# Folded weight pairs, quantised weight tiles and result buffers placed elsewhere in a two-layer attention and feed-forward kernel

## The chip, the cores and the metric

The kernel runs on one core of a Trainium2 chip. The metric is the device time of one execution in microseconds (us), as the median of three runs. Five engines work beside each other, each through its own list of instructions in order: TensorE (PE, with its weight loads shown as PEld), VectorE (DVE), ScalarE (ACT), GpSimd (POOL) and SyncE (SP), which in this kernel issues nearly all DMAs.

## The reference

The input x has 8 batches of 100 rows of 512 numbers, 800 rows in all. Two layers follow, each made of a cross attention and a feed-forward block that are added to x:

```python
x = x + L0_xattn(layernorm(x), ctx, Wq, Wkv_expand, Wout)      # 16 heads, causal
x = x + L0_ffn(layernorm(x), Wg, W1, W2, W3)                   # 8 experts, best 2 of 8
x = x + L1_xattn(layernorm(x), ctx, Wq, w_kc_q, w_kc_kv, W_qr, W_kr, Wo)
x = x + L1_ffn(layernorm(x), w_gate_up, w_down)                # quantised to 8 bits
```

In the second attention the queries pass through three matrices per head: `q_hk = hidden_q @ Wq.T`, then `w_kc_q` (from 128 to 384 numbers per head), then `W_qr` (from 384 to 64). In the second feed-forward block the rows, both weights and the hidden values are rounded to integers from -127 to 127, with one scale per row: `scale = max|v| / 127`, `q = round(v / scale)`, and `q * scale` is used.

## The kernel before

**Stages.** The 800 rows lie in 7 tiles of 128 (the last has 32). The kernel computes attention 1 batch by batch, then the gate (which two experts each row goes to), then the eight experts one after another on 240 slots each, then attention 2 batch by batch, then the last feed-forward block tile by tile. Each row goes to a slot of an expert through DRAM: `give_slots` works out the slots and POOL scatters the rows into `x_slot` (L686); `fetch` (L1015) reads an expert's slots back; the results are scattered with addition into `x_acc` (L1186).

**Order.** Up to the branch and in the expert loop the order on PE, DVE and ACT is the order in which the code is written (`tc.manual_schedule`). SP and POOL are ordered by a planner, and so is all of attention 2.

**The branch.** If an expert gets more than 240 rows, the rest is computed in a block under `tc.If(spills > 0)`. The number is worked out from the gate (`spilt`, L831), and each engine loads it and branches (L906, L913). In the profiled run the block is skipped.

**Folding.** The three query matrices of attention 2 are multiplied into one, `wqf`, two heads (one pair) at a time, eight pairs in all, as filler work ahead of attention 2. `fold_load(i)` (L698 to L705) brings a pair in by five DMAs from SP: `wq_p` of 512 KB, two `kq_p` of 192 KB and two `qr_p` of 96 KB. Then

- `fold_first` (L711): 6 matrix products of 128x64 on PE (12 records), and a copy to `a_p` by ACT (L719);
- `fold_second` (L749): 2 products of 64x512 (4 records), copied to `f_p` by ACT (L753);
- `fold_third` (L759): 4 transposes, copied to `wqf` by ACT (L760).

In the expert loop `fold_beside` (L731) and `fold_turn` (L741) take the place of `fold_first`. The pool of the loads has three buffers. Pairs 0 and 1 are folded among the gate's instructions ahead of the branch, pairs 2 and 3 directly behind the branch, pairs 4 to 7 in experts 0 to 3.

**The gate's second part.** Rows 640 to 799 (tiles 5 and 6) pass the gate last: statistics, `gate_norm` (L560), `gate_columns` (transposes L578, copies L583 and L581), `gate_scores` (L593, L601), `rank_choices` (a row of some 20 short DVE instructions with one exponential on ACT, L631), `give_slots` (products L658 and L661 on PE, then DVE and the scatters).

**An expert.** `gate_and_up(0)`, `(1)` and `(2)` each do 16 records L1109 on PE, a silu on ACT (L1120, L1128) and the product `hT` on DVE (L1121 to L1133). Then the next expert's rows are transposed (`columns_of`, L1040) and copied to `xgT`, one half by ACT (L1044) and one by DVE (L1042); then `hT` goes through the third weight (L1175), and the results are scaled (L1183, L1185) and scattered.

**Integers of the last block's weights.** Between these, DVE turns weights of the last feed-forward block into integers: `quantise` is a maximum (L147), two short instructions (L135, L138) and two passes (L142, L143), then SP sends the tile through a DMA that transposes it (L152). `quantise_next` does one of 22 gate/up tiles (128x512), twice per expert, and asks for the next (`gu`, L850); `quantise_down` does one of 4 down tiles (128x1408) in experts 0 to 3, between `gate_and_up(1)` and `(2)`, and `load_down` then asks for the next into the same buffer (`dn`, L855). `LATER = 9` of the gate/up tiles are left for attention 2, where up to two per batch from batch 1 on have a place.

**The end.** `finish_rows` scales a result (L1668), adds x (L1671) and sends it out (L1672), in buffers named `y`, of which there are two.

## Time and profile before

| | us |
|---|---|
| median of three runs | 674.64 |
| runs | 672.87 to 675.77 |
| profiled execution | 681.28 |
| its span | 679.5 |
| PE busy | 646.9 (95%) |
| DVE busy | 419.9 (62%) |
| ACT busy | 245.0 (36%) |
| POOL busy | 183.5 (27%) |

The stages of the profiled execution, by their first matrix products: attention 1 to about 105 us, the gate and the branch to 131, folded pairs to 141.6, experts 143.5 to 283, weights of the values and queries to 345, attention 2 to 536, the last block to 679.5.

Below, the page's slices: the span in 40 equal parts of 17 us. Each digit is the busy share of an engine in tenths (9 is 90% or more); PEclk is the clock granted to PE in tenths of full speed; DMA is the mean busy share of the DMA engines.

```profile
PE   8999997889998999999989999999999999999994
...
DVE  4875697326655553353148877876677356666687
ACT  3654544322222111232145555555555313222140
...
PEclk9999999589999999999989999999999999999998
DMA  9700393699999998654200211110000210011211
```

The eighth slice runs from 119 to 136 us, where the gate's second part, the branch and the first folded pairs behind it lie. The DMA engines are busy at 90% or more in the slices of the experts.

A row of a timeline gives the start in us, the length in us, the engine, the line, the operation, what it writes and reads, and in brackets how long the engine was idle before and what ended that.

### The profile page before, as it was taken

Reading aid. Unit: us, or ns where it says so; the run is one execution under the profiler, and the core shown is the slowest. Engines: PE = TensorE matmul, PEld = TensorE weight load, DVE = VectorE, ACT = ScalarE, POOL = GpSimd, SP = SyncE. Lnnn points to the kernel's source line nnn. Section 1 sums busy time; section 2 is a strip of 40 time slices with the busy share of each in tenths; the row PEclk is TensorE's granted clock in tenths of the full one; section 3 lists DMA queues with packets and bytes.
Section 4 is the critical chain, followed back from the end, with each engine's and each line's share of the span. In section 5 each row is a group of like instructions: output and inputs, shape, how many; then the busy total and the mean of one; then the engine's idle time right before and its main releaser. Section 6 shows DMA issues by size and latency. Waiting matters only on the chain.

```text
span 679.5 us, 9904 instructions
## 1 busy us (share of the span) xinstructions
PE 646.9 (95%) x3476; PEld 415.3 (61%) x3483; DVE 419.9 (62%) x1065; ACT 245.0 (36%) x565; POOL 183.5 (27%) x196
## 2 busy tenths in 40 slices
PE   8999997889998999999989999999999999999994
PEld 5766755666655677568866666666666544444442
DVE  4875697326655553353148877876677356666687
ACT  3654544322222111232145555555555313222140
POOL 2222231501110122138514243244234102221020
PEclk9999999589999999999989999999999999999998
DMA  9700393699999998654200211110000210011211
GB/s 292 249 18 17 119 322 108 241 309 220 299 295 302 253 326 214 140 175 120 84 1 15 59 44 21 53 36 12 0 13 0 90 38 20 18 30 29 49 37 63
DMA packets 80290, 80.35 MB, mean 118 GB/s; under 512 B 41267, under 2 KB 54119, under 8 KB 80111
## 3 DMA queue, kind: packets, MB, share of 16 engines
q1 hardware_dynamic: 76543, 70.97, 36.6%
q0 software_dynamic: 3696, 8.72, 6.0%
q8 instruction: 29, 0.48, 0.3%
q14 instruction: 22, 0.18, 0.1%
HBM read 56.36 MB, written 16.50 MB: 107 GB/s over the span
## 4 chain that ended last, share of the span: by engine, by line
PE 63%; DVE 7%; DMA 7%; POOL 1%; issue 1%; ACT 1%; SPq 0%; ACTq 0%; POOLq 0%; DVEq 0%
PE bank L359 12%; PE bank L1406 9%; PE bank L1379 9%; PE bank L1109 8%; PE bank L1325 6%; PE bank L1175 5%; PE bank L1394 5%; PE bank L1539 3%; DMA dn<-in_wdn 2%; PE bank L1361 1%; DMA gu<-in_wgu 1%; DMA qr_p<-in_wqr 1%; POOL e L1388 1%; DVE amax L147 1%; PE bank L711 1%
## 5 line engine op out<-in xcount | busy, mean ns | idle before, releaser
L1388 POOL TENSOR_SCALAR e<-e,rs 128x361 f32<-128x361 f32 (+1 forms) x56 | 67.2, 1201 | 131.9 <-DVE rs L1387 118.7
L359 PE MATMUL bank<-wvo,ctxT 128*128 128x512 f32 x192 | 83.9, 593 | 0.0
L1379 PE MATMUL bank<-kvT,qe 128*128 128x361 f32 (+1 forms) x208 | 83.0, 483 | 0.1
L1109 PE MATMUL bank<-xgT,w 128*128 128x240 f32 (+1 forms) x384 | 76.5, 373 | 1.6 <-ACT xgT L1044 0.9
L1109 PEld LDWEIGHTS bank<-xgT,w 128*128 128x128 f32 (+1 forms) x384 | 64.7, 183 | 14.4 <-issue 5.6
L1406 PE MATMUL bank<-pT,kvr 121*128 121x400 f32 x192 | 70.3, 502 | 1.0 <-DVE pT L80 1.0
L1394 PEld LDWEIGHTS bank<-ident,e 128*121 128x121 f32 (+1 forms) x312 | 48.3, 186 | 34.2 <-POOL e L1388 7.3
L1385 ACT ACTIVATE e<-bank,nm 128x361 f32<-128x361 f32 (+1 forms) x104 | 58.7, 565 | 27.2 <-DVE nm L1381 18.9
L1381 DVE TENSOR_REDUCE nm<-bank 128x1 f32<-128x361 f32 (+1 forms) x104 | 54.9, 528 | 15.8 <-PE bank L1379 14.6
L359 PEld LDWEIGHTS bank<-wvo,ctxT 128*128 128x128 f32 x192 | 36.2, 190 | 43.0 <-issue 42.6
L1186 POOL DMA_INDIRECT x_acc<-y,place x16 | 24.5, 1530 | 129.9 <-ACT y L1185 126.2
L1394 PE MATMUL bank<-ident,e 128*121 128x128 f32 (+1 forms) x312 | 53.0, 280 | 3.1 <-POOL e L1388 3.0
L1556 POOL TENSOR_TENSOR hid<-g,u 128x512 f32<-128x512 f32 (+1 forms) x17 | 20.5, 1216 | 111.0 <-ACT g L1547 74.8
L1175 PE MATMUL bank<-w,hT 128*128 128x512 f32 (+3 forms) x96 | 44.3, 607 | 4.0 <-DVE hT L1133 4.0
L1406 PEld LDWEIGHTS bank<-pT,kvr 121*128 121x128 f32 x192 | 33.9, 190 | 20.2 <-ACT pT L82 0.7
L1325 PE MATMUL bank<-xT,wqf 128*128 128x256 f32 (+1 forms) x192 | 43.8, 389 | 0.7 <-ACT xT L1310 0.7
L82 ACT COPY pT<-bank 121x384 f32<-121x384 f32 (+1 forms) x63 | 28.2, 447 | 42.4 <-PE bank L1394 42.3
L324 POOL TENSOR_TENSOR s<-s,rs 100x800 f32<-100x800 f32 x16 | 24.4, 1522 | 70.0 <-DVE rs L323 30.5
L1325 PEld LDWEIGHTS bank<-xT,wqf 128*128 128x128 f32 x192 | 36.3, 190 | 7.4 <-ACT xT L1310 0.9
L80 DVE COPY ctxT<-bank 128x400 f32<-128x400 f32 (+2 forms) x31 | 17.7, 572 | 37.0 <-PE bank L1325 26.0
L1379 PEld LDWEIGHTS bank<-kvT,qe 128*128 128x128 f32 (+1 forms) x208 | 32.9, 189 | 10.7 <-DVE rs L1387 0.5
L1175 PEld LDWEIGHTS bank<-w,hT 128*128 128x128 f32 (+3 forms) x96 | 16.8, 184 | 25.1 <-issue 16.6
(259 smaller groups left out, 1004.2 us busy)
## 6 DMA issues: line engine op xcount, KB each, us to landing
w<-in_w SPq DMA_DIRECT2D x8, 1408.0 KB
gu<-in_wgu SPq DMA_DIRECT2D x22, 256.0 KB
w<-in_w SPq DMA_DIRECT2D x16, 256.0 KB
wq_p<-in_wq SPq DMA_DIRECT2D x8, 512.0 KB
wo<-in_wo SPq DMA_DIRECT2D x8, 512.0 KB
x_slot<-zeros SPq DMA_DIRECT2D x1, 3840.0 KB
kq_p<-in_wkcq SPq DMA_DIRECT2D x16, 192.0 KB
dn<-in_wdn SPq DMA_DIRECT2D x4, 704.0 KB
```

What stands on the lines that cost most here:

```text
L82: nc.scalar.copy(dst, src)
L359: nc.tensor.matmul(po[:, :D], lhs[:, c, ds(t * P, r)], rhs[:, c, :], start=(c == 0), stop=(c == chunks - 1),)
L1109: nc.tensor.matmul(po, w12_e[:, c, cols], xgT[:, c, :], start=(c == c0), stop=(c == c1 - 1))
L1175: nc.tensor.matmul(py[i][:n], hT[:mr, m, ds(s0, n)], w3_e[:mr, m, :], start=(m == 0), stop=(m == 2))
L1186: d = nc.gpsimd.indirect_dma_start(out=x_acc, out_offset=bass.IndirectOffsetOnAxis(ap=place[:, 0:1], axis=0), in_=y, in_offset=None, compu ...
L1325: nc.tensor.matmul(pq[:, i, :], wqf[:, c, ts(p0 + i, P)], xT[:, c, :], start=(c == 0), stop=(c == KC - 1),)
L1379: nc.tensor.matmul(ps[:r, :L], qe[:, ds(k0, r)], kvT, start=True, stop=True)
L1381: d = nc.vector.tensor_reduce(nm[:r], ps[:r, :L], AX.X, ALU.max, negate=True)
L1385: nc.scalar.activation(e[:r], ps[:r, :L], AF.Exp, bias=nm[:r], accum_out=sm[:r])
L1388: (nc.vector if odd else nc.gpsimd).tensor_scalar_mul(e[:r], e[:r], rs[:r])
L1394: nc.tensor.transpose(pt[:LP, c, :r], e[:r, ds(c * (LP - 1), LP)], ident[:r, :r])
L1406: nc.tensor.matmul(pc[:, :VC], kvr[:, c, :], pT[:, c, :], start=(c == 0), stop=(c == LC - 1))
```

## The change

Four edits, in the same functions:

1. The fold loads have four buffers in place of three. Pairs 0 to 3 are loaded at the start and folded ahead of the branch, in pieces placed among the gate's second part. Pairs 4 and 5 are loaded there and folded behind the branch, now one after the other in their second and third steps. Pairs 6 and 7 are left for experts 0 and 1; both are loaded behind the branch at once.
2. `quantise_down` goes behind `gate_and_up(2)`, and from experts 0 to 3 to experts 1 to 4. `quantise_next`'s second tile still follows it.
3. 13 gate/up tiles are left for attention 2 in place of 9, so 9 are done in the experts.
4. `y` has four buffers.

To make room, the skipped block now uses memory of `x_all` and `xs` for its weights and rows; this is not shown.

```diff
-    fw, close_fw = open_pool("fold_in", bufs=3, side="right")
+    fw, close_fw = open_pool("fold_in", bufs=4, side="right")
...
-    pairs_left = list(range(3, NH1 // 2))
-    loaded = [fold_load(i) for i in range(3)]
+    pairs_left = list(range(4, NH1 // 2))
+    loaded = [fold_load(i) for i in range(4)]
...
-    part = fold_first(*loaded.pop(0))
+    pair0 = fold_first(*loaded.pop(0))
     project_add(5, po)
...
-    part = fold_second(*part)
+    pair0 = fold_second(*pair0)
     loaded.append(fold_load(pairs_left.pop(0)))
+    pair1 = fold_first(*loaded.pop(0))
     xT = gate_columns(5, 7)
-    fold_third(*part)
+    pair1 = fold_second(*pair1)
+    loaded.append(fold_load(pairs_left.pop(0)))
     gate_scores(5, 7, xT)
 
-    part = fold_first(*loaded.pop(0))
+    pair2 = fold_first(*loaded.pop(0))
+    fold_third(*pair0)
+    fold_third(*pair1)
     rank_choices(5, 7)
     give_slots(5, 7)
...
-    part = fold_second(*part)
-    fold_third(*part)
+    pair2 = fold_second(*pair2)
+    pair3 = fold_first(*loaded.pop(0))
+    fold_third(*pair2)
+    pair3 = fold_second(*pair3)
+    fold_third(*pair3)
...
-    LATER = 9
+    LATER = 13
...
-    while len(loaded) < 3:
+    behind_branch = [loaded.pop(0) for _ in range(2)]
+    while pairs_left:
         loaded.append(fold_load(pairs_left.pop(0)))
...
-    part = fold_first(*loaded.pop(0))
-    following = fold_first(*loaded.pop(0))
-    part = fold_second(*part)
-    following = fold_second(*following)
-    fold_third(*part)
-    fold_third(*following)
+    pair4, pair5 = fold_first(*behind_branch[0]), fold_first(*behind_branch[1])
+    pair4 = fold_second(*pair4)
+    fold_third(*pair4)
+    pair5 = fold_second(*pair5)
+    fold_third(*pair5)
...
-        if e < KC:
+        gate_and_up(2)
+        if 0 < e <= KC:
             turn_down(*quantise_down(*down_in))
-            if e + 1 < KC:
-                down_in = load_down(e + 1)
-        gate_and_up(2)
+            if e < KC:
+                down_in = load_down(e)
...
-        y = f2w.tile([P, D], F32, tag="y", name="y")
+        y = f2w.tile([P, D], F32, tag="y", name="y", bufs=4)
```

More of the change, by code (lines that the diff above doesn't have):

```diff
@@ L937, in tile_kernel @@
             )
+        w12_at = x_all.rearrange("p t w -> p (t w)")[:, : KC * 2 * HE]
+        w12_at = w12_at.rearrange("p (c h) -> p c h", c=KC)
         at_w = sp.tile([P, KC + 3], I32, tag="at_w", name="at_w")
@@ L953, in tile_kernel @@
             nc.gpsimd.iota(at_x, pattern=[[0, 1]], base=0, channel_multiplier=1)
-            w12_e = sp.tile([P, KC, 2 * HE], F32, tag="spw", name="spw")
+            w12_e = w12_at
             for c in range(KC):
                 gathered(w12_e[:, c, :], w12.rearrange("e d h -> (e d) h"), at_w[:, c : c + 1])
-            w3_e = sp.tile([P, 3, D], F32, tag="sp3", name="sp3")
+            w3_e = xs[1:4]
             for m, (m0, mr) in enumerate(HCH):
                 gathered(
-                    w3_e[:mr, m, :], w3.rearrange("e h d -> (e h) d"),
+                    w3_e[m][:mr], w3.rearrange("e h d -> (e h) d"),
                     at_w[:mr, KC + m : KC + m + 1],
@@ L965, in tile_kernel @@
             with tc.For_i(0, NT, 1, hint_engines=()):
-                x_t = sp.tile([P, D], F32, tag="spx", name="spx")
+                x_t = xs[4]
                 gathered(x_t, x_all_rows, at_x)
@@ L991, in tile_kernel @@
                     nc.tensor.matmul(
-                        py[:, :D], hT[:mr, m, :], w3_e[:mr, m, :], start=(m == 0), stop=(m == 2)
+                        py[:, :D], hT[:mr, m, :], w3_e[m][:mr], start=(m == 0), stop=(m == 2)
                     )
-                y_t = sp.tile([P, D], F32, tag="spy", name="spy")
+                y_t = xs[5]
                 nc.vector.tensor_scalar(y_t, py[:, :D], g_t, None, ALU.mult)
@@ L1092, in tile_kernel @@
     nc.scalar.activation(most, ln_eps, AF.Silu)
-    part = fold_first(*loaded.pop(0))
-    following = fold_first(*loaded.pop(0))
-    part = fold_second(*part)
-    following = fold_second(*following)
-    fold_third(*part)
-    fold_third(*following)
+    pair4, pair5 = fold_first(*behind_branch[0]), fold_first(*behind_branch[1])
[3 more added lines that the diff above has]
+    fold_third(*pair5)
+    part = None
     turned = columns_of(0, slots[0])
@@ L1665, in finish_rows @@
         if y is None:
-            y = f2w.tile([P, D], F32, tag="y", name="y")
+            y = f2w.tile([P, D], F32, tag="y", name="y", bufs=4)
         scale = swb[:, OT * P :]
@@ L1735, in tile_kernel @@
         finish_rows(u, pd, s)
-    y = f2w.tile([P, D], F32, tag="y", name="y")
+    y = f2w.tile([P, D], F32, tag="y", name="y", bufs=4)
     for cols in (slice(0, D // 2), slice(D // 2, D)):
```

## The prediction

> **What bounds it now.** I read the slices of the page first: TensorE (PE) is busy nearly everywhere, so a gain must be PE work removed or a stall removed. One stretch breaks the rule, where PEclk falls to 5. I then asked for busy time in windows of 3.41 us laid on that fall. Columns: window; its length; busy us of PE, PEld, DVE, ACT, POOL; granted clock; DMA share; GB/s.

> ```profile
> 114.27:117.68 3.41, 1.30 (x6) 0.28 (x5) 2.77 (x12) 2.15 (x4) 2.21 (x2) 1.00 0.45 122
> 117.68:121.09 3.41, 2.90 (x16) 2.13 (x20) 1.19 (x3) 2.38 (x5) 2.61 (x3) 0.50 0.97 287
> ...
> 131.33:134.75 3.42, 3.42 (x18) 3.42 (x17) 0.00 (x0) 1.07 (x3) 0.27 (x1) 0.50 0.34 82
> 134.75:138.16 3.41, 3.41 (x14) 2.06 (x15) 0.00 (x0) 0.27 (x1) 0.00 (x0) 0.50 0.76 234
> 138.16:141.57 3.41, 3.41 (x14) 1.71 (x11) 0.00 (x0) 1.67 (x3) 0.00 (x0) 0.50 1.04 324
> 216.67:220.08 3.41, 0.98 (x3) 0.49 (x4) 3.19 (x9) 0.00 (x0) 0.00 (x0) 1.00 1.10 345
> 220.08:223.49 3.41, 3.41 (x7) 1.78 (x6) 2.86 (x10) 0.69 (x1) 1.69 (x2) 0.50 1.04 397
> 667.22:670.63 3.41, 2.26 (x23) 1.79 (x24) 3.34 (x7) 0.48 (x1) 0.00 (x0) 1.00 0.02 5
> 670.63:674.05 3.42, 1.28 (x12) 0.89 (x10) 2.69 (x5) 0.00 (x0) 0.00 (x0) 1.00 0.41 153
> ```

> The chain of waits and the timeline give the other stalls:

> ```profile
> 131.02 5.37 PE bank L711 x24
> 136.48 4.65 DMA gu<-in_wgu
> 141.14 7.44 DMA qr_p<-in_wqr
> ```

> ```profile
> 213.39 1.62 DVE L147 TENSOR_REDUCE amax<-dn 128x1 f32<-128x1408 f32 x1 [4.69 <-DMA dn<-in_wdn]
> 219.10 2.85 PE L1175 MATMUL bank<-w,hT 96*128 96x512 f32 x4 [2.88 <-DVE hT L1133]
> 234.00 0.67 DVE L147 TENSOR_REDUCE amax<-gu 128x1 f32<-128x512 f32 x1
> 236.07 0.62 DVE L1042 COPY xgT<-bank 128x448 f32<-128x448 f32 x1
> 237.89 9.23 PE L1109 MATMUL bank<-xgT,w 128*128 128x240 f32 x48
> 672.71 0.75 DVE L1668 SCALAR_TENSOR_TENSOR y<-bank,sh,swb 128x512 f32<-128x512 f32 x1 [0.66 <-DMA out_y<-y]
> ```

> In experts 2 and 3 the down weights arrive late, DVE waits for them in its order, and the products hT behind them hold PE's L1175.

> **Pairs moved ahead of the experts.** The stretch from 115.92 (end of pair 0's L749) to 141.63 (first L1040), 25.7 us, held pair 0's third and pairs 1 to 3; now it holds pair 0's third and pairs 1 to 5, two more. A pair there costs PE, at half clock, 2.82 (L711) + 1.98 (L749) + 1.11 (L759) = 5.9 us; at full clock 1.52 + 1.08 + 0.55 = 3.15 (the last from transposes L578, 20 in 2.74). Two pairs: 11.8 or 6.3. Second and third now follow each other pair by pair, so three thirds wait for their f_p copy (ACT 0.58 and handing over): +2.0. Filled: pair 1's L711 lies in the 2.27 us in which PE waited for x_all at 115.92 to 118.19 (-1.5), and pair 3's L711 in the 0.7 before 128.89. At half clock throughout: 25.7 + 11.8 + 2.0 - 1.5 - 0.7 = 37.3, so L1040 starts at 153.2. At full clock throughout I add the same list in order and reach 140.2 (branch 1.0 us as at 130.02 to 131.02).

> Queued behind the new pieces: pair 1's a_p copy (0.27) stands before the gT copy on ACT, and two wqf copies stand before the exponential of rank_choices. At full clock both fit where DVE's chain ends anyway. At half clock L711 and two L759 (5.0 us) end after DVE wants L658 and the exponential: some 3.8 us for spilt, the last scatters on POOL and SP's fetch of slots (at 134.54); PE's folds are later still, so these cost nothing more. On SP two more fold loads run before the branch, among scatters; their 1.1 MB each may delay the fetch by 0 to 2 us; I take 0, since DMA is at 0.3 to 0.6 from 128 to 136.

> Cover: expert 0's L731 waited 0.29 + 0.91 us for pair 4's qr_p, landed at 148.6. Pair 6 takes its place in the queue behind the same bytes. So being early is worth nothing, and of being late 1.2 us are free.

> **Does the clock hold?** [...] Counting streamed columns (L711 at 46%), the dropped window holds 1.1 us and the one kept at 667.22 some 1.8. The new order offers about 1.8 over the old gap, 1.5 to 1.6 in windows between 119 and 124, and 0.9 to 1.3 across the branch (0.75 + 1.0 us of gaps, then 24 L711). I go by the rows: the clock is lost, most likely before the branch. In the middle of that stretch (122.8 instead of 117.68) 2.6 us run at full clock, and L1040 starts at 150.6: +9.0, less cover 1.2, plus 0.9 for half a slow window left in expert 0: **+8.7**.

> **Experts 1 to 4.** Pairs leave experts 2 and 3. The down integers take DVE 3.92 us (213.39 to 217.31) and now stand after hT, but still before the second gate/up tile (2.04) and L1042, which every L1109 of the next expert needs. After hT at 234.05: 3.92 + 2.04 + 0.62 ends at 240.6, while PE wanted 237.89: a new stall of 2.8 us in experts 2 and 3. In expert 1 pair 7's pieces give PE 1.3 us more: 1.5. In expert 4 no gate/up tile is left for the second place: 0.8. From windows set on L1109's starts, these experts took 17.45, 19.59, 21.67, 16.13 = 74.8 us, and a plain one (the next) 15.21. New: 18.95 + 18.0 + 18.0 + 16.0 = 70.9, **-3.9**. A 2.8 us gap puts a window under the limit in about 7 of 10 phases, at 1.7 us each (220.08): +2.4 for two. So -1.5 net (bounds -3.9 and -0.5). Expert 0 loses its down integers' wait: -0.25. The down tiles land 6 to 9 us after issue and have over 11 us from one use to the next, so I take them as in time; late ones cost 0 to 2.

> **Attention 2** takes four more gate/up tiles on DVE. Batch 2 with two tiles took 21.71 us, batch 6 with none 21.72 (between the context transposes L1285), batch 4 with one 21.99: +0.2 (0 to 0.6). Experts 4 to 6, which lose them, had PE unbroken: 0.

> **Result buffers.** The wait behind y's DMA is 0.66 us of DVE at the end, where DVE sets it: -0.66; the 2.00 us that the chain gives to that DMA overlaps the work before.

> **Sum**: +8.7 - 1.5 - 0.25 + 0.2 - 0.66 = +6.5. The profiled execution took 681.28 us with a span of 679.5; the median of the runs is 674.64, and I carry the difference over to it: 681.1.

> **Rivals.**
> - The clock falls only at the branch (24 L711 stream too little). L1040 at about 145.3: +3.7 - 1.2 + 0.9, the rest -2.2: +1.2, 675.8. For it: the thin windows there. Against: those at 119 to 124 are hardly fuller.
> - Faster: the clock holds to the experts. It decides if 0.9 to 1.3 us of streaming in a window suffices, or if busy time is what counts (1.6 us or more in any window). Nothing is gained before 148.6, so -2.2: 672.4; and if the 2.8 us gaps miss the grid too, 670.0. Against: the rows above; for: the dropped windows all had an idle of over 2 us.

> **Chances.** Lost before the branch 0.5, at it 0.28, held 0.22. Runs may differ, the grid being free of the kernel's start. The range leaves out the lower part of the last case and the worst of the first (all at half clock and late tiles): 671.5 to 685; the forecast's own is 677 to 685. This kernel's measurement tells 0.5% (3.4 us) from no change: faster 0.2 (half the held case, and some for a stall that I overrate), same 0.25, slower 0.55.

> **What would show it.** Right: PEclk at 5 over several slices between 120 and 152, first L1040 near 150; L1109 waiting for DVE xgT L1042 by 2 to 3 us in experts 2 and 3; no DVE wait for dn; no wait for out_y. Wrong: full clock through the branch, or L1109 starting on time because the down integers or the gate/up tile end sooner than PE's L1175.

## The result, and the profile after

The changed kernel took **682.67 us** (median of four runs, 680.47 to 686.76), the kernel before 673.75 us on the same chip (672.33 to 675.77): ratio **1.0124, 95% interval 1.0088 to 1.0161**, slower by some 8.9 us. The two profiled executions lie nearer together: spans of 679.5 us before and 682.8 us after. That gap between the profiled pair and the timed runs is a finding of its own, taken up below.

First the ahead-of-the-experts stretch: busy time of the changed kernel in windows on the grid of its clock changes (in this profile all of them, the later ones at 225.46, 228.87, 358.58, 361.99 and 679.43, lie whole multiples of 3.41 us apart). The columns are as before: window, length, busy us of PE, PEld, DVE, ACT, POOL, granted clock, DMA share, GB/s.

```profile
116.24:119.65 3.41, 2.55 (x22) 2.11 (x20) 2.40 (x6) 2.43 (x5) 2.65 (x3) 1.00 0.87 236
119.65:123.06 3.41, 2.84 (x15) 0.54 (x13) 0.29 (x1) 1.70 (x5) 2.64 (x3) 0.50 1.02 345
...
126.48:129.89 3.41, 3.41 (x23) 2.32 (x22) 1.14 (x11) 1.54 (x4) 1.58 (x2) 0.50 1.04 389
129.89:133.30 3.41, 3.37 (x22) 1.96 (x20) 2.37 (x15) 1.44 (x3) 1.66 (x2) 1.00 0.57 213
133.30:136.72 3.42, 1.84 (x15) 1.63 (x15) 0.00 (x0) 2.55 (x4) 1.19 (x2) 1.00 0.49 154
136.72:140.13 3.41, 3.41 (x18) 3.21 (x18) 0.00 (x0) 0.49 (x2) 0.00 (x0) 0.50 0.57 175
```

The clock is lost at 119.65, although PE was busy for 2.55 of the 3.41 us ahead of it and never idle for more than 0.86 us in a row. It comes back for two windows at 129.89, which was not foreseen, and is lost again at 136.72 until 153.78. The first columns of slots (L1050, before L1040) start at 147.08 in place of 141.63, and expert 0's first L1120 (before L1109) at 149.80 in place of 143.53: 6.3 us later.

Next the chain of waits in the experts (start, us, what). "Issue" is time for which this view names no cause.

```profile
187.22 1.36 issue
188.58 9.31 PE bank L1120 x48
...
204.03 2.68 issue
206.70 9.31 PE bank L1120 x48
...
222.15 2.68 issue
224.83 10.99 PE bank L1120 x48
...
241.96 0.60 issue
```

Four new stalls stand just ahead of the next expert's L1120. The third also costs clock: 10.99 us for 48 products instead of 9.31, with a granted clock of 0.50 from 225.46 to 228.87. The timeline of VectorE around the second stall tells its cause (start, us, engine, line, operation):

```profile
199.63 0.40 DVE L1144 TENSOR_TENSOR hT<-silu,up 64x240 f32<-64x240 f32 x1
199.96 1.60 DVE L147 TENSOR_REDUCE amax<-dn 128x1 f32<-128x1408 f32 x1
...
203.78 0.68 DVE L147 TENSOR_REDUCE amax<-gu 128x1 f32<-128x512 f32 x1
...
205.98 0.62 DVE L1052 COPY xgT<-bank 128x448 f32<-128x448 f32 x1
```

Behind the last hT stand the down weights' integers (199.96 to 203.78), a gate/up tile (to 205.98), and only then L1052, whose columns the L1120 at 206.70 needs. No wait for dn is left on VectorE. At the end of the kernel y's products no longer wait for out_y, where 0.66 us stood:

```profile
674.85 0.75 DVE L1679 SCALAR_TENSOR_TENSOR y<-bank,sh,swb 128x512 f32<-128x512 f32 x1
675.63 0.69 DVE L1682 TENSOR_TENSOR y<-y,x 128x512 f32<-128x512 f32 x1
676.24 0.74 DVE L1679 SCALAR_TENSOR_TENSOR y<-bank,sh,swb 128x512 f32<-128x512 f32 x1
```

### The profile page after: what moved, and what is told of

It is laid out like the page before. It is cut to its first block, busy times and chain, and to the rows that moved or that the text cites. A ratio compares the mean times of both kernels' runs of the same rounds, so it can differ in the third digit from the quotient of the medians.

```text
span 682.8 us, 9917 instructions
## 1 busy us (share of the span) xinstructions
PE 650.2 (95%) x3481; PEld 417.9 (61%) x3481; DVE 415.9 (61%) x1065; ACT 244.7 (36%) x563; POOL 184.1 (27%) x196
## 4 chain that ended last, share of the span: by engine, by line
PE 69%; DVE 4%; issue 2%; DMA 1%; POOL 1%; ACT 1%; SPq 0%; ACTq 0%; POOLq 0%; DVEq 0%
PE bank L359 11%; PE bank L1120 11%; PE bank L1417 10%; PE bank L1390 9%; PE bank L1336 6%; PE bank L1186 6%; PE bank L1405 5%; PE bank L1550 3%; PE bank L1372 2%; PE bank L1050 1%; POOL e L1399 1%; PE bank L749 1%; DMA cos_sb<-in_rope_cos 1%; DMA x_acc<-y,place 1%; PE bank L711 1%
## 5 line engine op out<-in xcount | busy, mean ns | idle before, releaser
L1120 PE MATMUL bank<-xgT,w 128*128 128x240 f32 (+1 forms) x384 | 78.6, 381 | 8.2 <-issue 7.3
L1120 PEld LDWEIGHTS bank<-xgT,w 128*128 128x128 f32 (+1 forms) x384 | 66.8, 188 | 21.6 <-issue 13.4
L1392 DVE TENSOR_REDUCE nm<-bank 128x1 f32<-128x361 f32 (+1 forms) x104 | 54.8, 527 | 13.0 <-PE bank L1390 11.8
L1567 POOL TENSOR_TENSOR hid<-g,u 128x512 f32<-128x512 f32 (+1 forms) x17 | 20.5, 1218 | 111.0 <-ACT g L1558 74.8
L1186 PE MATMUL bank<-w,hT 128*128 128x512 f32 (+3 forms) x96 | 43.0, 595 | 0.3 <-DVE hT L1144 0.3
L1132 DVE TENSOR_TENSOR hT<-silu,bank 128x240 f32<-128x240 f32 x16 | 6.5, 404 | 41.2 <-ACT silu L1131 41.2
```

The source lines that it names most:

```text
L1120: nc.tensor.matmul(po, w12_e[:, c, cols], xgT[:, c, :], start=(c == c0), stop=(c == c1 - 1))
L1186: nc.tensor.matmul(py[i][:n], hT[:mr, m, ds(s0, n)], w3_e[:mr, m, :], start=(m == 0), stop=(m == 2))
L1392: d = nc.vector.tensor_reduce(nm[:r], ps[:r, :L], AX.X, ALU.max, negate=True)
```

## The experiments

My theory: two separate losses, the clock ahead of the experts and the down weights' integers on VectorE, of which the prediction took the second as nearly balanced by the waits it removes. Rivals: only one of the two costs anything; or time won ahead of the experts is given back to late transfers. Every ratio is to the kernel before on the same chip. The runs fall into three sets, each on a chip of its own: the first four experiments (before took 678.57 us there); both kernels again, both remedies, and the old fold order with late integers (678.05); and the rest (677.95). A ratio is not the quotient of two medians and can differ from it by some 0.3%.

**Folds alone.** The changed kernel with all edits but the order of the pairs undone:

```
-    LATER = 13
+    LATER = 9
-        gate_and_up(2)
-        if 0 < e <= KC:
+        if e < KC:
             turn_down(*quantise_down(*down_in))
...
+        gate_and_up(2)
-        y = f2w.tile([P, D], F32, tag="y", name="y", bufs=4)
+        y = f2w.tile([P, D], F32, tag="y", name="y")
```

> Only the first edit (pairs and four load buffers); down integers, gate/up tiles and y as before. Clock theory: PEclk at half in parts of 119 to 154 us, the first L1120 products some 6 us later than before (about 149.5 instead of 143.5), of which the pairs taken out of experts 2 and 3 give back 4.4; the waits for the late down tiles stay or shrink: +1 to +5 us against before. Rival (PE work alone, 6.3 us at full clock, and the clock plays no part): no half clock beyond that of before, about +2 us. Rival (down integers cause all of the loss): 0 or faster by 4 us.

Measured: 682.6 us, ratio 1.0056 (1.0036 to 1.0077), +3.8 us. The pairs ahead of the branch lose more than they save later. PE ran at half clock from 119.97 to 160.93 in the profile, which speaks against the rival in which the clock plays no part.

**Everything but the folds.** The kernel before with the down integers behind the silu products, thirteen tiles left, four buffers:

```
-    LATER = 9
+    LATER = 13
-        if e < KC:
+        gate_and_up(2)
+        if 0 < e <= KC:
             turn_down(*quantise_down(*down_in))
...
-        gate_and_up(2)
+        y = f2w.tile([P, D], F32, tag="y", name="y", bufs=4)
```

> The change without its first edit: three load buffers and pairs as before, with the down integers behind the silu products, thirteen tiles left and four result buffers. Theory: no wait for dn any more (4.7 us of PE and one slow window of 1.7 gone), in their place L1109's starts wait for xgT by about 1.4 us in each of experts 1 to 3 (pairs are there) and 0.7 in expert 4, and 0.66 us less at the end: -2 us against before, between -4 and +1. Rival (down integers cause all of the loss): +5 us or more.

Measured: 683.38 us, ratio 1.0079 (1.0064 to 1.0093), +5.4 us. This is a miss of my theory: the rest of the change loses more than the folds. Its chain of waits:

```profile
185.70 1.36 issue
...
204.90 1.28 issue
...
224.03 1.28 issue
...
240.75 0.61 issue
```

The stalls are those of the changed kernel, 1.3 instead of 2.7 us where a pair still fills PE. They sum to 4.5 us.

**Down integers last.** The changed kernel, with the same instructions emitted behind the expert's results y, after the next expert's columns:

```
         gate_and_up(2)
-        if 0 < e <= KC:
-            turn_down(*quantise_down(*down_in))
-            if e < KC:
-                down_in = load_down(e)
...
         gates = gates_next
+        if 0 < e <= KC:
+            turn_down(*quantise_down(*down_in))
+            if e < KC:
+                down_in = load_down(e)
```

> The change with one block moved: the down integers stand behind the expert's results (L1194), so behind the copy xgT that the next expert waits for. Theory: the waits of 1.36, 2.68, 2.68 and 0.60 us and the slow window in expert 4 go, nothing else changes: 7.3 to 9 us faster than the change, about 674.5. Rival (experts 1 to 4 are held by DMA, not by DVE's order): the same waits appear at another instruction, gain under 3 us.

Measured: 680.77 us, ratio 1.0032 (1.0019 to 1.0046). Against the two measures of the change (1.0124 above, 1.0174 below) that is 6.2 or 9.6 us less, where 7.3 to 9 were expected. In its chain of waits the stalls are gone:

```profile
192.44 9.07 PE bank L1120 x48
201.51 0.97 PE bank L1050 x8
202.49 5.17 PE bank L1182 x12
207.65 9.07 PE bank L1120 x48
216.72 0.97 PE bank L1050 x8
```

PE goes from one expert to the next without a pause, 15.21 us apart (192.44 to 207.65). So neither the integers' work nor their DMA was the cost, but what was queued behind them.

**The clock held by products nobody reads.** The changed kernel with five more products, in the waits ahead of and behind the branch, whose result no instruction reads (the five calls are not shown):

```
+    def filler():
+        nc.tensor.matmul(
+            bank()[:, :D], ident, experts[0][0][:, 0, :D], start=True, stop=True
+        )
```

> The change with five more f32 products of 128x512 on PE whose results nobody reads (0.9 us each at full clock, 4.6 us of added work): behind L711 of pair 1, ahead of and behind L711 of pair 2, behind L749 of pair 3 and of pair 4. Clock theory (what counts in a window of 3.41 us is streamed columns, not busy time): the clock holds at full speed through the branch or is lost for one or two windows at most, and the first expert starts at about 143 to 146 instead of 149.8 in spite of the added work: 4 to 6 us faster than the change. Rival (added PE work is what costs): 3 to 5 us slower than the change. Rival (fetch of the slots on SP behind the scatters sets the start): within 1 us of the change.

Measured: 684.27 us, ratio 1.0089 (1.0072 to 1.0107). The mean clock of its profile is 0.987, against 0.960 to 0.973 in two profiles of the changed kernel, and the slots' columns start at 146.60. Whether that is a gain depends on the measure of the change: against 1.0124 it is 2.4 us less, less than expected, and against 1.0174, from a chip like this one, 5.8 us.

**Both kernels again.** In the first four experiments' profiles a copy on ScalarE comes late, which was on time in the first profiles of before and of the change (the last section). So both kernels were run once more on such a chip, as the measure for all the rest.

> The kernel before once more, unchanged, for its profile on the chip of the first four experiments, where its median is 678.57 us. Theory A (the first profile of before held stalls that its timed runs mostly lack: dn waits of 0.87 and 2.88 us in experts 3 and 4, a third clock drop at 220 us): a span of about 676 us, one of these stalls missing, experts 3 and 4 nearer 17.6 us apart than 19.67 and 20.55. Theory B (the stalls belong to before, and the chip differs elsewhere): the same spacing of experts, and the difference in the stage of the branch, where the other kernels on this chip show ScalarE's a_p copy 1.8 to 3.5 us late.

> The changed kernel on the chip of the experiments. If folds (+3.8 us) and the rest (+5.3 us) add up: about 687.5 us, ratio 1.013, as on the first chip (1.0124). If the parts cover one another (a stall behind a late stage is no stall): 682 to 684 us.

Measured: before 677.58 us (ratio to its own other runs 0.9996, 0.9974 to 1.0017), span 678.3; the change 691.92 us, ratio 1.0174 (1.0120 to 1.0227), span 690.6. The parts alone sum to 1.0056 + 0.0079 = 1.0135, inside both intervals of the whole (1.0088 to 1.0161 and this one): within these intervals the edits add up, and no cover of one by the other shows. The change's 691.92 us lies above both expectations. Its six runs also show how the time goes with the clock in one and the same kernel: five took 690.61 to 693.39 us at mean clocks of 0.960 to 0.972, and one took 683.99 us at 0.986. In before the first profile's waits for dn are gone. VectorE's timeline, first in the profile on which the prediction rests:

```profile
191.72 1.62 DVE L147 TENSOR_REDUCE amax<-dn 128x1 f32<-128x1408 f32 x1 [2.68 <-DMA dn<-in_wdn]
213.39 1.62 DVE L147 TENSOR_REDUCE amax<-dn 128x1 f32<-128x1408 f32 x1 [4.69 <-DMA dn<-in_wdn]
```

and then in this one:

```profile
194.52 1.61 DVE L147 TENSOR_REDUCE amax<-dn 128x1 f32<-128x1408 f32 x1
212.39 1.62 DVE L147 TENSOR_REDUCE amax<-dn 128x1 f32<-128x1408 f32 x1 [0.18 <-DMA dn<-in_wdn]
```

The bracket is the idle time before an instruction and what ended it: 2.68 us became nothing and 4.69 us became 0.18. Both expectations of the second profile (they count experts from 1) held a half: the waits are missing, as theory A has it, and the copy is late, as B has it; so the span hardly differs (679.5 and 678.3) for two different reasons.

**Both remedies together**, fillers and late integers, once for itself and once more beside the next run:

> The changed kernel with both remedies: down weights' integers behind the expert's results, and five products whose result nobody reads, which keep the clock. In the profiles the filler brought the first expert from 152.4 to 146.6 us (late by 5.8 us without it) and the late integers brought experts 1 to 4 to 15.2 us apart. Theory (two separate losses): 680.77 - 5.8 = 675 us, ratio 0.995 (0.991 to 0.999). Rival (the experts' weights or the slots' rows set the pace of the first experts, and time won ahead of them is given back): 679 to 681, ratio 1.000 to 1.003.

> The changed kernel with the filler products and the late down integers once more (0.9924 of before at first), as the measure for the next run on the same chip: 0.990 to 0.995 if it holds; over 0.997 if the first was this chip's luck.

Measured: 673.21 us, ratio **0.9924 (0.9894 to 0.9955)**, then 672.49 us, **0.9916 (0.9883 to 0.9950)**. This version beats both kernels, the kernel before by 5 us and the change, at 1.0174, by 2.5% or some 17 us. Each remedy gains beside the other: the fillers bring 1.08% where the integers are late (1.0032 to 0.9924), the late integers 1.65% where the fillers are in (1.0089 to 0.9924), both clear of the intervals. So there are two losses. Against the change without remedies the sizes are less certain, as its two measures differ: the fillers alone bring 0.35 or 0.85%, the late integers alone 0.92 or 1.42%, both 2.0 or 2.5%. The rival in which time won ahead of the experts is given back would have left 1.000 to 1.003, so it falls. The second profile's windows over the stretch where the change ran at half clock:

```profile
116.24:119.65 3.41, 3.41 (x24) 2.38 (x22) 2.29 (x6) 2.42 (x5) 2.53 (x3) 1.00 0.88 244
119.65:123.06 3.41, 2.65 (x19) 1.20 (x19) 0.61 (x4) 1.55 (x5) 2.76 (x3) 1.00 1.07 373
...
129.89:133.30 3.41, 3.05 (x10) 1.44 (x10) 1.68 (x12) 1.93 (x5) 0.00 (x0) 0.50 0.40 143
...
140.13:143.54 3.41, 3.11 (x28) 2.94 (x28) 0.00 (x0) 0.87 (x3) 0.00 (x0) 1.00 0.94 278
```

The clock stays full past 119.65 and is lost only from about 130 to 140, behind a wait of 3.43 us for the late copy. Slots' columns start at 148.17 in place of 152.82.

**The old fold order with the late integers**, and the same with fillers. The first diff is against the run with everything but the folds; the second, further down, adds calls of the same `filler`:

```
-        if 0 < e <= KC:
-            turn_down(*quantise_down(*down_in))
-            if e < KC:
-                down_in = load_down(e)
...
         gates = gates_next
+        if 0 < e <= KC:
+            turn_down(*quantise_down(*down_in))
+            if e < KC:
+                down_in = load_down(e)
```

> The kernel before with the fold order of before, the down weights' integers emitted behind the expert's results, thirteen tiles left for attention 2, four result buffers. Theory (the place of the integers, between the silu products and the next expert's columns, cost most of the +5.3 us of the run without folds): 683.38 - 7 = 676 us, ratio 0.997 (0.993 to 1.001). Rival (the thirteen tiles left for attention 2 cost it): 682 to 684, ratio 1.005 or more.

```
     loaded.append(fold_load(pairs_left.pop(0)))
+    filler()
+    filler()
     xT = gate_columns(5, 7)
...
+    filler()
+    filler()
     most = small.tile([P, 1], F32, tag="most", name="most")
...
     part = fold_second(*part)
+    filler()
     fold_third(*part)
```

> The fold order of before, late down integers, thirteen tiles left and four buffers (0.9969 at first), and five unread products in the waits ahead of the branch, whose windows had 1.43 and 0.17 of 3.41 us busy. Theory A (the lost clock is what the fold order costs or saves; without it moving pairs ahead is worth nothing): the first expert at about 141 in place of 145.2, the pairs in experts 2 and 3 still cost 2.4 us each: 673 to 675 us, ratio 0.993 (0.990 to 0.996), as the filled kernel with its folds moved. Theory B (pairs ahead of the branch are worth their 4.8 us once the clock holds): ratio above 0.997, four us behind the other.

Measured: 676.86 us, ratio 0.9969 (0.9945 to 0.9992), and 676.68 us, 0.9985 (0.9959 to 1.0010). The first meets its theory: moving the same integers from behind the silu products to behind the results is worth 1.1% of the run without folds. The second is inconclusive. Its time is where theory B wanted it, four us behind the version with moved folds, but the profile gives B less. From the first slots' columns to the last expert's it took 113.08 us (143.60 to 256.68), the other 107.19 (148.17 to 255.36), which is 5.9 us for the pairs, less 4.6 for the later start: 1.3 us. The remaining 2.9 us of the spans' difference (674.4 and 670.2) lie in attention 2, about 1 of them where its first batch lost its clock in one profile and not in the other (last section). And its fillers were badly placed: four records, 3.76 us at half clock, hold L749 to 129.29, though its a_p was copied by 127.30.

**Small edits alone.** The kernel before with LATER = 13 and four result buffers:

> The kernel before with thirteen tiles left for attention 2 and four result buffers alone. Theory (together they are worth -0.3 to -1 us, and the late integers of the run without folds did the rest of its gain): ratio 0.999 (0.997 to 1.001). Rival (they carry that gain by themselves, late integers being worth nothing against before): 0.996 to 0.998. If thirteen tiles are late in attention 2: above 1.002.

Measured: 678.29 us, ratio 0.9982 (0.9945 to 1.0019). No loss of over 0.2%; a gain isn't shown. Beside the run without folds (1.0079) it puts 1.0% on the place of the down integers alone.

**The gaps filled.** The changed kernel with two products behind the down products of experts 1 to 3:

```
+        if 0 < e < KC:
+            for _ in range(2):
+                nc.tensor.matmul(bank()[:, :D], ident, w3_e[:, 0, :], start=True, stop=True)
```

> The changed kernel with two unread products behind the down products of experts 1 to 3, where TensorE waits for the next expert's columns (1.36, 2.68 and 2.68 us). The wait for VectorE stays, the clock would not be lost behind it (expert 3 took 12.16 us in place of 9.31 for its 48 products in one profile). Theory (wait and clock are two prices): 2 to 4 us under the changed kernel, ratio 1.008 to 1.013 where the changed kernel has 1.0174. Rival (the clock behind the waits costs next to nothing in most runs): 1.0124 to 1.018.

Measured: 689.98 us, ratio 1.0175 (1.0136 to 1.0213), no better than the change's 1.0174, though the median is 2 us lower. In the profiles the clock behind the gap is kept, as this pair of PE rows shows, the changed kernel's (the second run) first:

```profile
213.11 12.16 PE L1120 MATMUL bank<-xgT,w 128*128 128x240 f32 x48 [2.68 <-issue]
```

```profile
212.99 9.31 PE L1120 MATMUL bank<-xgT,w 128*128 128x240 f32 x48 [0.96 <-issue]
```

That is 2.85 us in one expert of one profile (spans 690.6 and 688.5), and nothing in the ratios. These are known to 0.4 and 0.5% either way, so what the clock behind the gaps costs in a typical run stays open.

## Why the prediction was right, and where it was not

Forecast 681.1, measured 682.67: the direction, the range and the two mechanisms hold. By its own steps:

- **The clock is lost before the branch**, by the rows and not by the busy time: right, at 119.65. The count of streamed columns behind it is not confirmed: it put about 1.8 us into the window over the old gap, as much as into the one kept at 667.22, and it was behind this window that the clock fell. "L1040 starts at 150.6" was 147.08 in the first profile, because the clock returned at 129.89 for two windows, and 152.82 in the second, where it did not. For "+8.7" the two pairs of profiles give +6.3 (143.53 to 149.80) and +8.6 (146.99 to 155.54). That the second is so near is in part luck: a late copy on ScalarE (last section) holds PE for 3.74 us in before and 1.68 in the change ahead of it. The pairs' departure from two experts is worth twice 17.6 less 15.2 us, so these terms give 8.7 - 4.8 = +3.9 for the folds; alone they measured +3.8, on a chip with the late copy. The rival in which the clock holds fell, and the fillers show its worth: when it holds longer the loss shrinks, by 1.08% beside the late integers.
- **New stalls of 1.5, 2.8, 2.8 and 0.8 us** ahead of the next expert's products: 1.36, 2.68, 2.68 and 0.60, from the cause named, as the late integers prove by removing them.
- **Clock behind the gaps, +2.4 for two**: one was lost in each of the two profiles of the change, at 1.7 and 2.85 us. Filling the gaps didn't settle it.
- **Attention 2, +0.2**: from the first batch's context transposes to the eighth's it is 161.24 us before (344.48 to 505.72) and 160.75 after (349.22 to 509.97), 161.51 and 160.93 in the second pair: 0.5 us less, so no cost of the four more tiles shows. **Buffers, -0.66**: the wait is gone; in time neither is told from nothing.
- **The step that failed is "so -1.5 net" for experts 1 to 4.** Its new side was right: 70.9 + 2.4 = 73.3 us for the four, measured 73.1 and 74.3 (169.45 to 242.56, 175.86 to 250.14). Its old side, "74.8" (75.0 by the starts of L1109), held the late dn of one execution. In the second profile of before the same four took 68.0 us (168.45 to 236.48), without these waits:

```profile
168.45 3.40 PE L1109 MATMUL bank<-xgT,w 128*128 128x240 f32 x16
236.48 9.23 PE L1109 MATMUL bank<-xgT,w 128*128 128x240 f32 x48
```

In the second profile of the change they took 74.3:

```profile
175.86 3.40 PE L1120 MATMUL bank<-xgT,w 128*128 128x240 f32 x16
250.14 9.31 PE L1120 MATMUL bank<-xgT,w 128*128 128x240 f32 x48 [0.60 <-issue]
```

So the stage lost 6.2 us there instead of gaining 1.5, and the stalls that the change "removes" were not there to remove. Small edits alone, with the folds and down integers of before, is a third profile: 69.4 us (164.80 to 234.17), with one wait for dn of 1.96 us on VectorE. So dn is sometimes late, and what it costs in a typical run is between nothing and the 7 us of the first profile; that it is near the low end is argued from the other two, as the timed runs left no traces. The profiled pair agrees with the forecast (-1.9), which shows only that it began from the same execution. Before's profiled execution took 681.28 us and its median was 674.64; the text carried the difference over as a constant, where it should have asked which rows of the profile made it; the 7.0 us between the two profiles' experts are about as much.
- The sum came out near all the same. By the second pair of profiles the -1.5 was 7.7 us too kind; against it stand the first chip's stretch ahead of the experts, 6.3 and not 8.7, and the wide intervals (the same change measured 1.0124 and 1.0174). It is a right total with a term of the wrong sign.

## What to carry to other kernels

When work is moved on an engine that runs in order, list everything behind its new place up to the next instruction that another engine needs: the same instructions cost about 1% behind the silu products and nothing measurable behind the results (without the folds 1.0079 and 0.9969). When the profiled execution is well above the median, here by 6.6 us, a wait for a transfer in it may not be in typical runs; a gain that consists of removing such a wait needs a second profile first. Work moved into a stretch at half clock cost nearly twice its time there: a pair's 12 L711 took 2.82 us in place of 1.52, its four L749 1.98 in place of 1.08. Five products that nobody reads cost less than the clock they kept (1.08% less time beside the late integers); where two of them stood ahead of a product that was ready, they held it for 2 us (127.30 to 129.29 in the filled old order).

## What the runs showed of the hardware

**Busy time alone did not hold the clock.** The change lost it behind a window with 2.55 us busy (12 of L711 with 64 columns, 8 transposes, 2 of L749). Attention 2's first batch kept it with 1.69 and lost it with 1.14. Small edits alone, then the filled old order, in windows on the grid of each profile's clock changes:

```profile
347.32:350.73 3.41, 1.69 (x10) 1.33 (x10) 1.62 (x9) 1.11 (x5) 1.74 (x2) 1.00 0.00 0
350.73:354.14 3.41, 2.95 (x16) 2.03 (x15) 2.83 (x9) 2.50 (x8) 2.04 (x2) 1.00 0.00 0
```

```profile
344.59:348.00 3.41, 1.14 (x7) 0.71 (x6) 1.55 (x6) 1.85 (x8) 1.40 (x1) 1.00 0.00 0
348.00:351.41 3.41, 3.41 (x11) 2.38 (x10) 2.21 (x8) 1.31 (x4) 1.46 (x2) 0.50 0.00 0
```

The same wait of 2.27 us for POOL stands here in all fourteen profiles, and the clock of the next window went with where it fell on the grid: with 2.13 us or more of it in one window the clock fell (eleven profiles), with 1.72 or less in one window it stayed (three). The grid was not tied to the kernel's start: the first fall in before is at 117.68 in one profile and at 119.39 in the other, 1.71 us later, while the L711 ahead of it starts 0.57 us later (112.97, 113.54). From the end of that wait to the first product with pT it took 4.89 us in the one and 5.85 in the other (349.04 to 353.93, 347.18 to 353.03). By these two, 0.96 us apart, an edit anywhere ahead can move the time by about a microsecond that has nothing to do with it (an estimate).

The runs give no limit in busy time even for wide products: the second profile of the change lost the clock at 212.08 behind 1.76 us of L1186, with 512 columns, where 1.69 us kept it above:

```profile
208.67:212.08 3.41, 1.76 (x5) 0.43 (x3) 3.24 (x7) 0.69 (x1) 1.50 (x1) 1.00 1.04 384
```

**A copy that starts late.** ScalarE's a_p copy behind the branch's scores started at once in the first profile of before and 4.2 us late in the second; PE's L711, from which it copies, had ended at 125.57 in the one and at 125.73 in the other:

```profile
125.61 0.27 ACT L719 COPY a_p<-bank 128x128 f32<-128x128 f32 x1 [3.65 <-PE bank L711]
```

```profile
129.89 0.27 ACT L719 COPY a_p<-bank 128x128 f32<-128x128 f32 x1 [7.76 <-remote]
```

VectorE's ranking came behind it (L648 at 126.01 in the one and at 130.29 in the other, there after 4.23 us of waiting for ScalarE's L631), then the slots' fetch (L1015 at 134.54 in the one, not before 136 in the other), and PE waited for it. PE's next L749 in the second profiles of before and of the change:

```profile
130.21 1.98 PE L749 MATMUL bank<-wq_p,a_p 128*64 128x512 f32 x4 [3.74 <-ACT a_p L719]
```

```profile
130.56 1.98 PE L749 MATMUL bank<-wq_p,a_p 128*64 128x512 f32 x4 [1.68 <-ACT a_p L719]
```

The copy was late, by 2.7 to 5.2 us, in each of the twelve experiments' profiles, of whatever kernel, but in neither of the first two, and before's medians were 4 us longer on those chips (678 for 673.75). The rows name `remote` as its releaser (eight) or a product of PE that had ended 1.3 to 1.4 us before (four); what it is stays open. All kernels on these chips share it, but they do not pay the same for it: PE waited 3.74 us in before and 1.68 in the change. So it can move a ratio by some 0.3% (an estimate: the 2.06 us between these two, over 678), and what follows on the clock's grid besides.
